# The second attention's last two key heads: folding their weights at the third head instead of beside the feed-forward

## The chip, the cores and the metric

The kernel runs on one NeuronCore of a Trainium2 chip. A core has a matmul engine (TensorE, called PE in the profile), a vector engine (VectorE, DVE), a scalar engine (ScalarE, ACT), a general one (GpSimd, POOL) and SyncE (SP), which here only issues DMAs. Each engine works through its own queue in order, and semaphores tie the queues together. PE writes only to PSUM, and ACT or DVE has to copy from there.

The metric is the device time of one execution in microseconds; the median of a few runs is compared. The profile is one further execution with the hardware profiler on, so its times sum to its own time.

## The reference

Two decoder layers on x of 4 x 256 tokens of width 256, each a gated cross-attention to a context (4 x 1601 tokens of width 128) and a gated feed-forward:

```python
x = x + tanh(g_xattn[0]) * L0_xattn(layernorm(x), ctx)   # 16 heads of 16
x = x + tanh(g_ffn[0])   * L0_ffn(layernorm(x))          # 16 experts, 8 chosen per token, and a shared one
x = x + tanh(g_xattn[1]) * L1_xattn(layernorm(x), ctx)   # 16 query heads of 128, 8 key heads
x = x + tanh(g_ffn[1])   * L1_ffn(layernorm(x))          # weights rounded to -1, 0, 1 times a scale
```

The second attention, which the change is about:

```python
q = (x @ Wq) in 16 heads of 128;  k, v = (ctx @ Wk), (ctx @ Wv) in 8 heads of 128, each for 2 query heads
attn = softmax(mask(q @ k.T / sqrt(128)))
out = concat(attn @ v) @ Wo
```

Since k = ctx Wk, a head's scores are x (Wq_h Wk^T) ctx^T, and since v = ctx Wv, its output is (attn ctx) (Wv Wo_h). The kernel makes the two small products once per head ("folding"): aq (256 x 128) and vo (128 x 256), and attends to ctx itself.

## The kernel before

The kernel runs in four stages, one after the other: first attention, first feed-forward (from 536 us on), second attention (from 638 us on), second feed-forward. Within a stage a Python loop writes the instructions out, and `keep_order` ties every engine to that order, except SP in the first feed-forward.

**First feed-forward.** It takes 512 tokens at a time ("half") and 16 experts for each, so 32 experts' turns, called slots 0 to 31. A turn (`expert`) is three products on PE into PSUM (`ps_v` L1279, `ps_g` L1280, `ps_w` L1281), a ReLU on ACT (L1235), two products on DVE (L1239, L1241) and one on POOL (L1242), which gives hT. After each second expert `add_pair` multiplies the previous pair's hT by the third weight (L1293). Other work is put beside the experts by slot, in the table `beside`: layer norms, routing, the second attention's context and mask (`prepare_ctx`, `prepare_mask`), the output tiles (L1303, L1304), and `fold_steps`, the folding of the second attention's weights.

**Folding.** A query head takes two steps. The first, called A in the text that follows, transposes the head's two blocks of Wq (L1211) and, for the first of the two query heads of a key head, also Wk and Wv (L1214) into one PSUM tile; ACT copies them out as kvT (L1216) and, scaled, qwT (L1218). The second, B, makes the two blocks of aq (L1224) and vo (L1227) in another PSUM tile; ACT copies aq (L1228), DVE vo (L1229). The 32 steps of 16 heads stand in slots 6 to 32, five slots with two. Wk, Wv and Wq are loaded to the memory of the first attention's keys (`space`), Wo to a tile of its own (`wo1`), by SP (L1182 to L1187); the context follows on the same queue (`ctxT`, L1192).

**Second attention.** Its units are (batch, head), 64 in all. The loop over v works on several at a time: the scores of unit v in eight tiles (PE L1457; DVE subtracts from the mask and finds the extremum, L1464; ACT takes the exponential, L1472), then the softmax factors (`weigh_sets`: DMAs L1483 to bring the parts of a query together, DVE L1486 and L1488, ACT L1489, DVE L1492 to L1495, DMAs L1498 back), then POOL multiplies (L1507), DVE transposes (`turn`, L1513), PE sums over the context (`attend`, L1520), ACT copies (`take`, L1530) and PE projects with vo (`project_out`, L1538). `project(v + 2)` (L1446, copied by ACT at L1447) makes the queries two units ahead, in one of two PSUM buffers named `ps_m`. The DMAs L1483 and L1498 are issued half by SP and half by ACT. For the first three units nothing is left to sum yet, or only little: at v = 2 PE finishes the third head's scores and goes on to the first head's sums, which need the first head's transposes.

At v = 2 the order on ACT is: the exponentials of the third head, the two DMAs L1483, the exponential L1489, two DMAs L1498, `take`, the copy of the queries. On DVE the transposes of the first head stand behind the score tiles of the third one.

In the background the loop quantises the last stage's weights: `fetch` loads 512 columns at a time into `w_q` (two buffers), one step every second unit, from v = 5 on.

Of the kernel before, what the change touches and what calls it, by code (L numbers as in the profile page):

```python
# [9 lines left out]
F32 = mybir.dt.float32  # L10
# [3 lines left out]
AF = mybir.ActivationFunctionType  # L14
# [7 lines left out]
P = 128  # L22
B, S, D = 4, 256, 256
NT = B * S // P
QT = S // P
DC = D // P
# [6 lines left out]
H = 16  # L33
# [26 lines left out]
def tile_gated_cross_blocks(ctx: ExitStack, tc: tile.TileContext, a: dict, out: bass.AP):  # L60
# [1072 lines left out]

    def prepare_ctx(b, pst, tag):

        cx = contexts[b] = l1w.tile([P, NB1, P], F32, name="cx1", bufs=2)
        for g0 in range(0, NB1, 4):
            n = min(4, NB1 - g0)
            cg = l1w.tile([P, 4, SETS, TQ], F32, name="cg")
            for i in range(SETS):  # L1140
                k0 = i * KS + g0 * TQ
                nc.gpsimd.tensor_copy(
                    cg[:, :n, i, :], ctxT[b][:, k0 : k0 + n * TQ].rearrange("p (k q) -> p k q", q=TQ)
                )
# [28 lines left out]
    with ExitStack() as ph:  # L1173
        began = len(nc.cur_bb.bb.instructions)
        space = kTs_f[(B - 1) % 2]
        at1 = NKV * HD1
        wk1, wv1 = space[:, :at1], space[:, at1 : 2 * at1]
        wq1 = space[:, 2 * at1 : 2 * at1 + DC * H * HD1].rearrange("p (c n) -> p c n", c=DC)
        fp = ph.enter_context(tc.tile_pool(name="l1f", bufs=1))
        ft = ph.enter_context(tc.tile_pool(name="l1ft", bufs=2))  # L1180
        wo1 = fp.tile([P, H, D], F32, name="wo1")
        nc.sync.dma_start(out=wk1, in_=a["L1_xattn_Wk"])  # L1182
        nc.sync.dma_start(out=wv1, in_=a["L1_xattn_Wv"])
        for h in range(0, H, 4):
            cols = slice(h * HD1, (h + 4) * HD1)
            nc.sync.dma_start(out=wq1[:, :, cols], in_=a["L1_xattn_Wq"].rearrange("(c p) n -> p c n", p=P)[:, :, cols])
            nc.sync.dma_start(out=wo1[:, h : h + 4], in_=a["L1_xattn_Wo"].rearrange("(h p) n -> p h n", p=P)[:, h : h + 4])  # L1187
            if h == 4:
                first_mask = prepare_mask(0)
                next(first_mask)  # L1190
        for b in range(B):
            nc.sync.dma_start(out=ctxT[b][:, :S2], in_=a["ctxT"][:, b, :])  # L1192
            nc.gpsimd.memset(ctxT[b][:, S2:], 0.0)
# [10 lines left out]
        def fold_steps():  # L1204
            for kv in range(NKV):
                cols = slice(kv * HD1, (kv + 1) * HD1)
                for r in range(GRP):
                    h = kv * GRP + r
                    pt = ps_x.tile([P, 512], F32, name="ps_x")
                    for c in range(DC):  # L1210
                        nc.tensor.transpose(pt[:, c * P : (c + 1) * P], wq1[:, c, h * HD1 : (h + 1) * HD1], ident)  # L1211
                    if r == 0:
                        for i, w in enumerate((wk1, wv1)):
                            nc.tensor.transpose(pt[:, (DC + i) * P : (DC + i + 1) * P], w[:, cols], ident)  # L1214
                        kvT = ft.tile([P, 2, P], F32, name="kvT")
                        nc.scalar.copy(kvT.rearrange("p i c -> p (i c)"), pt[:, DC * P :])  # L1216
                    qwT = ft.tile([P, DC, P], F32, name="qwT")
                    nc.scalar.activation(  # L1218
                        qwT.rearrange("p c d -> p (c d)"), pt[:, : DC * P], AF.Copy, scale=1.0 / math.sqrt(HD1)
                    )  # L1220
                    yield
                    pm = ps_x.tile([P, 512], F32, name="ps_x")
                    for c in range(DC):
                        nc.tensor.matmul(  # L1224
                            pm[:, c * P : (c + 1) * P], lhsT=qwT[:, c, :], rhs=kvT[:, 0, :], start=True, stop=True
                        )
                    nc.tensor.matmul(pm[:, DC * P :], lhsT=kvT[:, 1, :], rhs=wo1[:, h, :], start=True, stop=True)  # L1227
                    nc.scalar.copy(aq[:, :, h, :], pm[:, : DC * P].rearrange("p (c d) -> p c d", c=DC))  # L1228
                    nc.vector.tensor_copy(vo[:, h, :], pm[:, DC * P :])  # L1229
                    yield  # L1230
# [85 lines left out]
        follow(fold_steps(), sorted([*range(6, 33), 7, 14, 17, 22, 25]))  # L1316
# [23 lines left out]
        for step in beside.pop(32):  # L1340
            step()
# [15 lines left out]
    with ExitStack() as ph:  # L1357
# [20 lines left out]
        def quantise():  # L1378
# [4 lines left out]
            def fetch(k):  # L1383
                i, j = todo[k % len(todo)]
                w = got[k] = ap.tile([P, FC], F32, name="w_q", bufs=2)
# [5 lines left out]

            asum = small.tile([P, len(todo)], F32, name="asum", bufs=1)
# [17 lines left out]
            for k, (i, j) in enumerate(todo):  # L1410
# [3 lines left out]
                below = ap.tile([P, FC], F32, name="q_dn")  # L1414
# [173 lines left out]
        for v in range(len(units) + 8):  # L1588
# [13 lines left out]
            if v - 3 in made:  # L1602
                project_out(v - 3)
            if v - 2 in made:
                if early:
                    for half in range(2):
                        turn(v - 2, half)
                for k in range(NB1):
                    attend(v - 2, k)
# [133 lines left out]
```

## Time and profile before

| what | value |
|---|---|
| median of 3 runs | 1567.58 us (1565.86 to 1568.48) |
| the profiled execution's own time | 1567.33 us |
| its span | 1565.6 us |
| PE busy | 1523.9 us, 97% |
| DVE, ACT, POOL busy | 71%, 51%, 36% |
| mean granted clock of PE | 0.995 |
| share of PE in the chain that ended last | 88% |

Times in the timeline are microseconds from the start of the span. A row is a run of instructions of one line and shape: start, time, engine, line, operation, tiles, shapes, count, and in brackets how long the engine had been idle before and what ended that. A matmul's time includes the way through the array, so that the next one starts before it ends; where instructions follow closely, the distance from one start to the next is what an instruction costs. A row of a table of windows has the bounds of the stretch, its length, the busy time of PE, PEld (weight loads), DVE, ACT and POOL with the number of instructions, the granted clock of PE (1.00 is full), the busy share of the DMA engines, and GB/s.

### The profile page before, as it was taken

The page shows a single profiled execution, that of the slowest core. Times are in us where ns is not written, and L with a number is a line of the kernel's source. Part 1 is how long each engine was busy: PE and PEld are TensorE (multiplying, and loading weights), DVE is VectorE, ACT ScalarE, POOL GpSimd, SP SyncE. Part 2 cuts the span into 40 slices and gives each one's busy share as a digit, 9 for nine tenths or more (in the row PEclk, how much of TensorE's full clock was granted, in tenths as well). Part 3 has the DMA queues.
Part 4 walks back from the last instruction along what each step waited for, and adds up shares of the span by engine and source line. Part 5 has one row for each costly group of instructions (what it writes and reads, how often), then busy time and mean ns, then how long its engine had stood idle before and what let it go on. Part 6 is the DMA issues. An engine that isn't in the chain of part 4 may idle for free.

```text
span 1565.6 us, 31791 instructions
## 1 busy us (share of the span) xinstructions
PE 1523.9 (97%) x12210; PEld 924.1 (59%) x12218; DVE 1104.2 (71%) x2559; ACT 795.4 (51%) x2017; POOL 563.1 (36%) x454
## 2 busy tenths in 40 slices
PE   8999999999999999899999999999999999999998
PEld 5455555555555544366666666666666666666655
DVE  7666676676567367677777777777787777777655
ACT  4456556566555544534445445454445554454343
POOL 4142022032012245244445444454444544444400
PEclk9999999999999999999999999999999999999999
DMA  5120003003200410000000000000000000000000
GB/s 144 24 51 1 1 2 64 1 2 56 46 15 15 146 54 1 2 2 15 9 23 8 16 10 15 9 15 9 9 16 9 22 9 16 9 2 2 2 0 28
DMA packets 47596, 34.48 MB, mean 22 GB/s; under 512 B 31058, under 2 KB 42196, under 8 KB 47316
## 3 DMA queue, kind: packets, MB, share of 16 engines
q1 hardware_dynamic: 33732, 31.22, 8.2%
q10 hardware_dynamic: 13712, 1.23, 0.6%
q8 instruction: 96, 1.57, 0.4%
q14 instruction: 56, 0.46, 0.1%
HBM read 30.16 MB, written 1.46 MB: 20 GB/s over the span
## 4 chain that ended last, share of the span: by engine, by line
PE 88%; DVE 4%; ACT 4%; issue 2%; POOL 1%; DMA 1%; ACTq 0%; SPq 0%; DVEq 0%; POOLq 0%
PE ps_o L1520 21%; PE ps_sc L1457 20%; PE ps_s L801 9%; PE ps_g L758 7%; PE ps_o L827 7%; PE ps_y L1538 4%; PE ps_m L1446 3%; PE ps_v L1279 2%; ACT pr L1472 1%; PE ps_m L586 1%; PE ps_a L1293 1%; ACT e L812 1%; PE ps_m L493 1%; PE ps_m L734 1%; PE ps_g L1651 1%
## 5 line engine op out<-in xcount | busy, mean ns | idle before, releaser
L1507 POOL TENSOR_TENSOR pr<-pr,rs 128x1604 f32<-128x1604 f32 x128 | 364.0, 2865 | 434.1 <-DMA rs<-ws 387.8
L1520 PE MATMUL ps_o<-pT,cx 128*128 128x256 f32 x1664 | 371.5, 381 | 8.6 <-DVE pT L1513 8.6
L1457 PE MATMUL ps_sc<-ctxT,qT 128*32 128x401 f32 x4096 | 359.7, 502 | 0.5 <-DVE nm L1464 0.5
L1464 DVE CUSTOM_DVE_ANT_0 pr<-ps_sc,mk 128x401 f32<-128x401 f32 x512 | 293.8, 576 | 88.7 <-PE ps_sc L1457 50.6
L1472 ACT ACTIVATE pr<-pr,nm 128x401 f32<-128x401 f32 x512 | 321.1, 628 | 69.0 <-DVE nm L1464 68.5
L1520 PEld LDWEIGHTS ps_o<-pT,cx 128*128 128x128 f32 x1664 | 317.8, 191 | 52.6 <-DVE pT L1513 9.7
L812 ACT ACTIVATE e<-ps_s 128x512 f32<-128x512 f32 x430 | 222.3, 565 | 166.6 <-PE ps_s L801 158.1
L767 DVE TENSOR_REDUCE mxs<-ps_g 128x1 f32<-128x453 f32 x372 | 216.5, 623 | 112.1 <-PE ps_s L801 81.0
L801 PE MATMUL ps_s<-qT,kT 32*128 32x256 f32 x1600 | 250.8, 403 | 11.2 <-ACT e L812 9.9
L1457 PEld LDWEIGHTS ps_sc<-ctxT,qT 128*32 128x32 f32 x4096 | 126.5, 110 | 204.4 <-issue 120.5
L1513 DVE STREAM_TRANSPOSE pT<-pr 128x1664 f32<-128x1664 f32 x128 | 242.9, 1899 | 5.4 <-POOL pr L1507 5.3
L758 PE MATMUL ps_g<-kT,qT 32*128 32x453 f32 (+1 forms) x992 | 244.0, 539 | 1.4 <-DVE mxs L767 1.1
L801 PEld LDWEIGHTS ps_s<-qT,kT 32*128 32x128 f32 x1600 | 151.6, 185 | 89.6 <-ACT e L812 49.1
L1489 ACT ACTIVATE ws<-ws 32x32 f32<-32x32 f32 x64 | 14.6, 228 | 198.7 <-DVE ws L1488 198.7
L827 PE MATMUL ps_o<-e,vp 128*32 128x256 f32 x1664 | 114.3, 388 | 0.0
L1530 ACT COPY ao<-ps_o 128x256 f32<-128x256 f32 x64 | 23.8, 372 | 151.9 <-PE ps_o L1520 130.2
L1472 ACT ACTIVATION_READ_ACCUMULATOR pr<-pr,nm 128x1 f32 x512 | 95.5, 187 | 0.0
L758 PEld LDWEIGHTS ps_g<-kT,qT 32*128 32x128 f32 x992 | 90.0, 184 | 8.4 <-DVE mxs L767 7.7
L827 PEld LDWEIGHTS ps_o<-e,vp 128*32 128x32 f32 x1664 | 43.4, 110 | 62.1 <-issue 45.5
L1538 PE MATMUL ps_y<-vo,ao 128*128 128x256 f32 x256 | 72.4, 405 | 0.1
L1538 PEld LDWEIGHTS ps_y<-vo,ao 128*128 128x128 f32 x256 | 43.4, 189 | 44.4 <-ACT pr L1472 39.8
L1486 DVE TENSOR_REDUCE low<-bq 32x8 f32<-32x32 f32 x64 | 12.4, 194 | 75.9 <-DMA bq<-nm 75.9
(325 smaller groups left out, 1533.8 us busy)
## 6 DMA issues: line engine op xcount, KB each, us to landing
kT<-by_head SPq DMA_DIRECT2D x64, 93.3 KB, 4.6
ctxT<-in_ctxT_dram SPq DMA_DIRECT2D x4, 800.5 KB, 9.8
ctx<-in_ctxT_dram SPq DMA_DIRECT2D x12, 199.0 KB, 4.7
kT<-in_L_xattn_Wq_dram SPq DMA_DIRECT2D x4, 512.0 KB, 3.6
wo<-in_L_xattn_Wo_dram SPq DMA_DIRECT2D x4, 512.0 KB, 5.2
bq<-nm SPq DMA_DIRECT2D x128, 2.0 KB, 1.7
bq<-nm ACTq DMA_DIRECT2D x128, 2.0 KB, 2.0
rs<-ws SPq DMA_DIRECT2D x128, 1.0 KB, 1.9
```

What stands on the lines that cost most here:

```text
L758: nc.tensor.matmul(ps[:, m * w : (m + 1) * w], lhsT=qT[rows, ii * P : (ii + 1) * P], rhs=kT[rows, s // 2, n * CW0 : n * CW0 + w], start=Tr ...
L767: nc.vector.tensor_reduce(mx[:, i, r + k, n : n + 1], ps[:, :w], AX.X, ALU.max)
L801: nc.tensor.matmul(ps[:, jj * S : (jj + 1) * S], lhsT=kT[rows, s // 2, (j + jj) * P : (j + jj + 1) * P], rhs=qT[rows], start=True, stop=True,)
L812: nc.scalar.activation(e[:, k, : nj * S], ps[:, : nj * S], AF.Exp)
L827: nc.tensor.matmul(summed[u][(r + k) * W : (r + k + 1) * W, :S], lhsT=vps[b % 2][:, t, h * VW : h * VW + W], rhs=made[u, j, r][:, k, jj * ...
L1457: nc.tensor.matmul(ps[i * TQ : (i + 1) * TQ, :KS], lhsT=queries[u][:, t * TQ : (t + 1) * TQ], rhs=ctxT[b][:, i * KS : (i + 1) * KS], start ...
L1464: nc.vector.tensor_tensor_reduce(out=prs[u % 3][:, t, :KS], in0=ps[:, :KS], in1=masks[b], scale=-1.0, scalar=3.0e38, op0=ALU.add, op1=ALU. ...
L1472: nc.scalar.activation(p, p, AF.Exp, bias=found[u][:, 0, t : t + 1], scale=-1.0, accum_out=found[u][:, 1, t : t + 1])
L1507: nc.gpsimd.tensor_tensor(p, p, bc_last(factors[:, ts], KS), ALU.mult)
L1513: nc.vector.transpose(pTs[u % 2][:, ts].rearrange("p t k -> p (t k)"), prs[u % 3][:, ts].rearrange("p t k -> p (t k)"))
L1520: nc.tensor.matmul(po[:, u % 2], lhsT=contexts[b][:, k, :], rhs=pTs[u % 2].rearrange("p t (k q) -> p t k q", q=TQ)[:, :, k, :], start=k == ...
L1538: nc.tensor.matmul(ys[b][:, i], lhsT=outs[u][:, i * P : (i + 1) * P], rhs=vo[:, h, :], start=(h, i) == (0, 0), stop=(h, i) == (H - 1, QT - 1),
```

## The change

The weights of the last two key heads (four of the sixteen query heads, `LATE` = 2) are loaded to tiles of their own (`lkv`, `lq`, `lo`) and folded in the second attention's loop at v = 2, between the third head's scores and the first head's sums. For these four heads the fold's PSUM tiles are `ps_m`, its copies kvT and qwT have one buffer, and ACT copies vo too. The other twelve heads are folded beside the feed-forward as before, 24 steps in slots 6 to 8 and 10 to 30. Half of Wo (eight heads) now lies in `space` too. The quantising uses `lq` and `lkv` in place of `w_q` and `q_dn`.

```diff
+    LATE = 2
+    late = l1_stack.enter_context(tc.tile_pool(name="late", bufs=1, side="right"))
+    lkv = late.tile([P, 2, LATE, HD1], F32, name="lkv")
+    lq = late.tile([P, DC, LATE * GRP, HD1], F32, name="lq")
+    lo = late.tile([P, LATE * GRP, D], F32, name="lo")
+
+    def load_late():
+        h0, kv0 = H - LATE * GRP, NKV - LATE
+        for i, n in enumerate(("Wk", "Wv")):
+            nc.sync.dma_start(
+                out=lkv[:, i], in_=a[f"L1_xattn_{n}"][:, kv0 * HD1 :].rearrange("p (h n) -> p h n", n=HD1)
+            )
+        for c in range(DC):
+            nc.sync.dma_start(
+                out=lq[:, c],
+                in_=a["L1_xattn_Wq"][c * P : (c + 1) * P, h0 * HD1 :].rearrange("p (h n) -> p h n", n=HD1),
+            )
+        nc.sync.dma_start(out=lo, in_=a["L1_xattn_Wo"].rearrange("(h p) n -> p h n", p=P)[:, h0:])
+
+    def fold(kv, r, kT_of, q_of, o_of, pst, tag, pool, memo):
+
+        h = kv * GRP + r
+        pt = pst.tile([P, 512], F32, name=tag)
+        for c in range(DC):
+            nc.tensor.transpose(pt[:, c * P : (c + 1) * P], q_of(c, h), ident)
+        if r == 0:
+            for i in range(2):
+                nc.tensor.transpose(pt[:, (DC + i) * P : (DC + i + 1) * P], kT_of(i, kv), ident)
+            memo[kv] = pool.tile([P, 2, P], F32, name="kvT")
+            nc.scalar.copy(memo[kv].rearrange("p i c -> p (i c)"), pt[:, DC * P :])
+        kvT = memo[kv]
+        qwT = pool.tile([P, DC, P], F32, name="qwT")
+        nc.scalar.activation(qwT.rearrange("p c d -> p (c d)"), pt[:, : DC * P], AF.Copy, scale=1.0 / math.sqrt(HD1))
+        yield
+        pm = pst.tile([P, 512], F32, name=tag)
+        for c in range(DC):
+            nc.tensor.matmul(pm[:, c * P : (c + 1) * P], lhsT=qwT[:, c, :], rhs=kvT[:, 0, :], start=True, stop=True)
+        nc.tensor.matmul(pm[:, DC * P :], lhsT=kvT[:, 1, :], rhs=o_of(h), start=True, stop=True)
+        nc.scalar.copy(aq[:, :, h, :], pm[:, : DC * P].rearrange("p (c d) -> p c d", c=DC))
+        eng = nc.scalar.copy if kv >= NKV - LATE else nc.vector.tensor_copy
+        eng(vo[:, h, :], pm[:, DC * P :])
+        yield
...
-        for h in range(0, H, 4):
+        for h in range(0, HE, 4):
             cols = slice(h * HD1, (h + 4) * HD1)
             nc.sync.dma_start(out=wq1[:, :, cols], in_=a["L1_xattn_Wq"].rearrange("(c p) n -> p c n", p=P)[:, :, cols])
-            nc.sync.dma_start(out=wo1[:, h : h + 4], in_=a["L1_xattn_Wo"].rearrange("(h p) n -> p h n", p=P)[:, h : h + 4])
+            nc.sync.dma_start(out=wo1[h // 8][:, h % 8 : h % 8 + 4], in_=a["L1_xattn_Wo"].rearrange("(h p) n -> p h n", p=P)[:, h : h + 4])
             if h == 4:
                 first_mask = prepare_mask(0)
                 next(first_mask)
+        load_late()
...
-        follow(fold_steps(), sorted([*range(6, 33), 7, 14, 17, 22, 25]))
+        follow(fold_steps(), [*range(6, 9), *range(10, 31)])
...
-                w = got[k] = ap.tile([P, FC], F32, name="w_q", bufs=2)
+                w = got[k] = w_q[:, k % 2]
...
+            w_q = lq.rearrange("p c h n -> p (c h n)").rearrange("p (k n) -> p k n", n=FC)
+            below = lkv.rearrange("p i h n -> p (i h n)")
...
-                below = ap.tile([P, FC], F32, name="q_dn")
...
             if v - 3 in made:
                 project_out(v - 3)
+            if v == 2:
+                memo = {}
+                for kv in range(NKV - LATE, NKV):
+                    k = kv - (NKV - LATE)
+                    for r in range(GRP):
+                        for _ in fold(
+                            kv, r,
+                            lambda i, kv: lkv[:, i, k],
+                            lambda c, h: lq[:, c, h - (H - LATE * GRP)],
+                            lambda h: lo[:, h - (H - LATE * GRP)],
+                            ps_m, "ps_m", ap, memo,
+                        ):
+                            pass
             if v - 2 in made:
```

More of the change, by code (lines that the diff above doesn't have):

```diff
@@ L1175, in tile_gated_cross_blocks @@
         space = kTs_f[(B - 1) % 2]
-        at1 = NKV * HD1
+        HE = H - LATE * GRP
+        at1, at2 = HE // GRP * HD1, 2 * (HE // GRP) * HD1 + DC * HE * HD1
         wk1, wv1 = space[:, :at1], space[:, at1 : 2 * at1]
-        wq1 = space[:, 2 * at1 : 2 * at1 + DC * H * HD1].rearrange("p (c n) -> p c n", c=DC)
+        wq1 = space[:, 2 * at1 : at2].rearrange("p (c n) -> p c n", c=DC)
         fp = ph.enter_context(tc.tile_pool(name="l1f", bufs=1))
         ft = ph.enter_context(tc.tile_pool(name="l1ft", bufs=2))
-        wo1 = fp.tile([P, H, D], F32, name="wo1")
-        nc.sync.dma_start(out=wk1, in_=a["L1_xattn_Wk"])
-        nc.sync.dma_start(out=wv1, in_=a["L1_xattn_Wv"])
-        for h in range(0, H, 4):
+        wo1 = [
+            space[:, at2 : at2 + 8 * D].rearrange("p (h n) -> p h n", n=D), fp.tile([P, HE - 8, D], F32, name="wo1")
+        ]
+        nc.sync.dma_start(out=wk1, in_=a["L1_xattn_Wk"][:, :at1])
+        nc.sync.dma_start(out=wv1, in_=a["L1_xattn_Wv"][:, :at1])
+        for h in range(0, HE, 4):
             cols = slice(h * HD1, (h + 4) * HD1)
             nc.sync.dma_start(out=wq1[:, :, cols], in_=a["L1_xattn_Wq"].rearrange("(c p) n -> p c n", p=P)[:, :, cols])
-            nc.sync.dma_start(out=wo1[:, h : h + 4], in_=a["L1_xattn_Wo"].rearrange("(h p) n -> p h n", p=P)[:, h : h + 4])
+            nc.sync.dma_start(out=wo1[h // 8][:, h % 8 : h % 8 + 4], in_=a["L1_xattn_Wo"].rearrange("(h p) n -> p h n", p=P)[:, h : h + 4])
             if h == 4:
@@ L1204, in fold_steps @@
         def fold_steps():
-            for kv in range(NKV):
-                cols = slice(kv * HD1, (kv + 1) * HD1)
+            memo = {}
+            for kv in range(NKV - LATE):
                 for r in range(GRP):
[L1208 to L1219, printed above, removed]
-                    )
[L1221 to L1230, printed above, removed]
+                    yield from fold(
+                        kv, r,
+                        lambda i, kv: (wk1, wv1)[i][:, kv * HD1 : (kv + 1) * HD1],
+                        lambda c, h: wq1[:, c, h * HD1 : (h + 1) * HD1],
+                        lambda h: wo1[h // 8][:, h % 8, :],
+                        ps_x, "ps_x", ft, memo,
+                    )
         def squared_relu_times(dst, pg, pv, pw=None):
@@ L1339, in tile_gated_cross_blocks @@
             waiting = (half, e, hTs)
-        for step in beside.pop(32):
+        for step in beside.pop(32, []):
             step()
@@ L1603, in tile_gated_cross_blocks @@
                 project_out(v - 3)
+            if v == 2:
+                memo = {}
+                for kv in range(NKV - LATE, NKV):
+                    k = kv - (NKV - LATE)
+                    for r in range(GRP):
+                        for _ in fold(
+                            kv, r,
+                            lambda i, kv: lkv[:, i, k],
[4 more added lines that the diff above has]
+                            pass
             if v - 2 in made:
```

## The prediction

> **What bounds the kernel now.** I read the busy shares first, then who TensorE waited for, then the two stretches that the change touches, in order of time. TensorE (PE) is busy 97% of the span, so a stretch of it costs what it does there plus what it waits there. From the page:
>
> ```profile
> PE 1523.9 (97%) x12210; PEld 924.1 (59%) x12218; DVE 1104.2 (71%) x2559; ACT 795.4 (51%) x2017; POOL 563.1 (36%) x454
> ```
>
> Only one wait of PE in the second attention is large (line; total us, times, longest):
>
> ```profile
> PE ps_o L1520 <- DVE pT L1513: 8.6, 2, 8.1
> ```
>
> The timeline shows it between the third head's scores (L1457) and the first sums (L1520). In brackets is the idle time and what ended it; the last row is the same work one head later.
>
> ```profile
> 655.51 5.59 PE L1457 MATMUL ps_sc<-ctxT,qT 128*32 128x401 f32 x64
> 669.16 7.60 PE L1520 MATMUL ps_o<-pT,cx 128*128 128x256 f32 x26 [8.06 <-DVE pT L1513]
> 684.05 5.78 PE L1520 MATMUL ps_o<-pT,cx 128*128 128x256 f32 x26
> ```
>
> PE ends at 661.10 and starts at 669.16, 8.06 us. The first sums take about 2 us more than the next ones (7.60 in the chain against 5.61), and the windows say why: the clock (the last but two column here) had fallen.
>
> ```profile
> 661.00:665.00 4.00, 0.10 (x4) 0.00 (x0) 3.08 (x9) 3.73 (x13) 2.25 (x1) 1.00 0.00 0
> 665.00:669.00 4.00, 0.00 (x0) 0.00 (x0) 4.00 (x4) 0.72 (x2) 1.16 (x1) 0.61 0.04 2
> 669.00:673.00 4.00, 3.83 (x10) 3.10 (x11) 2.77 (x4) 0.23 (x1) 4.00 (x2) 0.54 0.01 1
> ```
>
> From 674 on PE never waits for long, so what is later at the end of the first sums (676.76) is later at the end of the kernel. The question is when ScalarE (ACT), which has to empty every PSUM tile of the fold, gets to it in this gap. ACT in the timeline:
>
> ```profile
> 649.36 1.48 ACTq L1483 DMA_DIRECT2D bq<-nm  x2
> 650.88 0.37 ACT L1447 COPY qT<-ps_m 128x256 f32<-128x256 f32 x1 [1.56 <-PE ps_sc L1457]
> ...
> 667.02 0.19 ACT L1472 ACTIVATION_READ_ACCUMULATOR pr<-pr,nm 128x1 f32 x1
> 667.24 1.42 ACTq L1483 DMA_DIRECT2D bq<-nm  x2
> ```
>
> ACT works on the third head's exponentials until 667.21 and then issues two DMAs, which hold it for 1.42 us: after the issue at 649.36 the next copy starts at 650.88, though its matmul had ended at 649.0. So ACT is free at 668.66, 7.6 us after the scores and half a microsecond before PE's wait ends.
>
> **What is removed from the feed-forward.** A head is two steps: A, transposes of Wq (and Wk, Wv for a key head's first query head), and B, three products. PE from one start to the next:
>
> ```profile
> 618.84 0.44 PE L1211 MATMUL ps_x<-ident,kT 128*128 128x128 f32 x2
> 619.12 0.38 PE L134 MATMUL ps_x<-ident,xn 128*128 128x128 f32 x2
> ...
> 621.71 0.71 PE L1224 MATMUL ps_x<-kvT,qwT 128*128 128x128 f32 x4
> 622.26 0.60 PE L1227 MATMUL ps_x<-wo,kvT 128*128 128x256 f32 x2
> 622.69 0.38 PE L134 MATMUL ps_x<-ident,xn 128*128 128x128 f32 x2
> ...
> 624.27 0.44 PE L1211 MATMUL ps_x<-ident,kT 128*128 128x128 f32 x2
> 624.55 0.38 PE L1214 MATMUL ps_x<-ident,kT 128*128 128x128 f32 x2
> 624.86 1.08 PE L1293 MATMUL ps_a<-hT,kT 128*64 128x512 f32 x4
> ...
> 632.37 1.79 PE L1293 MATMUL ps_a<-hT,kT 128*64 128x512 f32 x4
> ```
>
> A is 0.28 us for a second head, 0.59 for a first one; B is 0.98. Four heads are 2 x 0.59 + 2 x 0.28 + 4 x 0.98 = 5.7 us. Not all of it is saved. The last head's A and B (slots 31 and 32) lie in the shadow of the last expert's chain: PE ends its product at 629.56, then follow ACT, DVE and POOL (its product ends at 633.03), and only then the last L1293, whose 1.79 us is mostly waiting. Taking 0.28 + 0.98 us from there makes PE wait longer. So 15 heads in slots 6 to 30 become 12: 2 x 0.59 + 0.28 + 3 x 0.98 = 4.40 us saved.
>
> Is PE the limit in those slots? An expert without any filler ran at 1.63 us (starts at 538.48, 540.11, 541.78, each 0.20 to 0.23 us of waiting for DVE); with filler it is 1.27 plus the filler. Every slot keeps a step or other work, the smallest being A with 1.27 + 0.28 + 0.09, and odd slots have L1293 (1.0 us) as well. So 4.40 holds, at worst 2.4 if DVE, busy 69% at 600 to 620, holds two slots per head. DVE's four vo copies (0.33 us each) go; they bound nothing.
>
> Loads: the same bytes in three more DMAs on SP's queue. The five late ones wait for the transposes at 532.2 (L866) and are issued in SP's idle time before 535.67, ahead of the last Wo part, the mask and ctxT on that queue. After 535.67 SP then issues one Wo part instead of four at about 0.5 us each, so ctxT, first read at 552.14 on POOL, comes no later. POOL's order is unchanged. The second attention's quantising reads the same amounts into lq instead of w_q, with two halves as before; its only new wait is for transposes long done. Cost: 0. Without this cover a late ctxT would hold POOL, and each hT behind it, one for one.
>
> **What is added at the third head.** All on PE and ACT, in their written order, 14 ACT instructions between the DMAs at 667.24 and the factors' exponential (L1489). PE does the first A at once, 661.1 to 661.9, and then waits for ACT. ACT's pace and the way from B to the copy are those beside the feed-forward:
>
> ```profile
> 554.10 0.71 PE L1224 MATMUL ps_x<-kvT,qwT 128*128 128x128 f32 x4
> ...
> 555.28 0.37 ACT L1228 COPY aq<-ps_x 128x256 f32<-128x256 f32 x1 [0.65 <-PE ps_x L1227]
> 555.55 0.39 ACT L1218 ACTIVATE qwT<-ps_x 128x256 f32<-128x256 f32 x1
> ```
>
> B's start to the aq copy is 1.18 us; copies start 0.27 apart; qwT takes 0.39 and PE follows 0.05 later. kvT at 668.70, qwT 668.97, so B of the first head starts at 669.41. From one B to the next: 1.18 + 0.27 (aq) + 0.27 (vo, now on ACT too) + 0.44 = 2.16 us, and 0.27 more for kvT at a new key head, 2.43. PE's transposes for the next head fit between. The four: 669.41 + 2.16 + 2.43 + 2.16 + 0.98 = 677.14, PE free for the first sums. They are no longer hidden by the gap: nearly all of the fold comes after its end.
>
> The clock adds to it. In the trace it falls at about 665.9 whatever follows, so the first B runs at half speed: by transposes at that clock (four in 1.04 us at 53.43, against 0.53) and sums (0.43 us against 0.22) B takes 1.96 and the copy comes 1.03 later. How long it stays low no row shows, since PE is here busy only about 75% of each 2.3 us. At the least one head is slow, 1.03 us; with two, and the four transposes between them (0.46 more), 2.5; with all four, 4.6. The Trainium skill (TensorE: Matmul & The Clock Gate, "The HAM clock gate") has full speed return after a window of about 3.4 us of sustained activity, and be lost after an idle one. The rows agree for solid work: 669.16 to 672.66, 3.5 us. But they also show a stretch that wasn't idle and lost it:
>
> ```profile
> 47.90:51.40 3.50, 1.34 (x6) 0.67 (x6) 1.29 (x5) 2.65 (x7) 0.00 (x0) 1.00 0.03 7
> 51.40:54.90 3.50, 3.48 (x20) 2.35 (x24) 1.29 (x3) 1.37 (x3) 0.00 (x0) 0.51 0.00 0
> ```
>
> 38% busy was too little. Read strictly, "sustained" keeps the clock low through the fold and into the sums; 75% is nearer to solid work than to 38%, so I take 1.6 us, between one and two heads. The sums then start at 678.7 and run at full speed, 5.61, to 684.3, against 676.76: 7.6 us later.
>
> Queued behind the fold on ACT is L1489 (670.77 before, some 679.6 now). DVE waits there at L1492, and behind that are the transposes of the second head and the DMA of the third head's factors, for which POOL waits. The second head's transposes then end at 684.5, and its sums are due at 684.3 + 0.86 + 5.52 + 1.06 = 691.7, so nothing more is late.
>
> Sum: -4.4 + 7.6 = +3.2 us against the profiled execution's 1567.33 (span 1565.6), which is 0.25 below the median of the runs: 1570.5 there, 1570.8 as a median.
>
> **Rivals.**
> - The clock stays low through the fold: 677.14 + 4.6 + 7.60 = 689.3, 12.6 later, less 4.4: +8.2, 1575.8. For it: the 38% row. Against it: the fold's PE is nearly twice as busy.
> - The feed-forward saves only 2.4 because DVE and ACT set the pace: +5.2, 1572.8. Against it: PE shows no wait from 560 to 620.
> - Not slower: a DMA issue doesn't hold ACT's copies. Then kvT starts at 667.24 and all is 1.42 earlier: +1.8, 1569.4. Against it: three pairs like 649.36 and 650.88.
> - Faster, the gap takes the fold: ACT would serve the copies between the exponentials, and the 4.4 us are a plain gain, 1563.2. It decides if the fold ends before 675.55 (676.76 + 4.4 - 5.61), 3.1 us earlier than I have it. Against it: ACT's order, in which the copies stand behind the exponentials and the DMAs.
>
> **How the numbers follow.** This kernel's measurement tells about 0.2%, 3.1 us, from no change; the forecast lies on that edge. Main case 60% (1569.8 to 1572.0, half on each side), low clock 15%, slow feed-forward 10%, early copies 7%, faster 6%, anything else 2%. Slower: 30 + 15 + 10 + 2 = 57%; same 29 + 7 = 36%; faster 7%. The range leaves out the faster case and the upper half of the low clock: 1568.2 to 1575.5.
>
> **What would show it.** Right: PE shows the first transposes right after the third head's scores and then a wait of about 7 us for ACT; the first fold copy starts 1.4 us after the last exponential; four heads about 2.2 to 3.2 us apart; the first sums in 5.6 us, not 7.6; the feed-forward 4.4 us shorter. Wrong: copies before the DMA issue, a clock at 0.5 up to the sums, new waits of PE for DVE in the feed-forward, or the second head's sums waiting for DVE.

## The result, and the profile after

The changed kernel takes 1572.78 us (median of 7 runs, 1572.16 to 1574.05) against 1567.58 (7 runs beside it, 1565.61 to 1568.48): a ratio of 1.0037, 95% interval 1.0026 to 1.0049. It is slower by more than the 0.2% that this kernel's measurement can tell. The profiled execution took 1572.16 us, with a span of 1570.4.

The busy shares of the page have hardly moved, so they say nothing of the cause:

```profile
PE 1525.9 (97%) x12210; PEld 924.4 (59%) x12218; DVE 1101.0 (70%) x2555; ACT 796.9 (51%) x2021; POOL 563.2 (36%) x454
```

The largest wait of PE in the second attention has a new place. In the list of waits (line; total us, times, longest), 9.4 us now lie ahead of the fold's products, 7.4 of them in one piece, and the 8.1 us wait of the first sums for DVE is 0.5:

```profile
PE ps_m L1170 <- ACT qwT L1166: 9.4, 4, 7.4
PE ps_o L1553 <- DVE pT L1546: 0.5, 1, 0.5
```

PE's timeline at the third head (L1490 scores, L1158 and L1161 transposes, L1170 and L1171 products of the fold, L1553 sums):

```profile
650.64 5.59 PE L1490 MATMUL ps_sc<-ctxT,qT 128*32 128x401 f32 x64
656.17 0.44 PE L1158 MATMUL ps_m<-ident,lq 128*128 128x128 f32 x2
656.44 0.38 PE L1161 MATMUL ps_m<-ident,lkv 128*128 128x128 f32 x2
664.26 1.23 PE L1170 MATMUL ps_m<-kvT,qwT 128*128 128x128 f32 x4 [7.44 <-ACT qwT L1166]
...
667.37 1.22 PE L1170 MATMUL ps_m<-kvT,qwT 128*128 128x128 f32 x4 [0.60 <-ACT qwT L1166]
...
671.04 1.23 PE L1170 MATMUL ps_m<-kvT,qwT 128*128 128x128 f32 x4 [0.75 <-ACT qwT L1166]
...
674.15 1.22 PE L1170 MATMUL ps_m<-kvT,qwT 128*128 128x128 f32 x4 [0.60 <-ACT qwT L1166]
...
676.01 6.71 PE L1553 MATMUL ps_o<-pT,cx 128*128 128x256 f32 x26
682.56 1.03 PE L1479 MATMUL ps_m<-xnT,aq 128*128 128x256 f32 x4
```

PE does the first transposes at once, then waits until ACT has copied them. The four heads begin 3.11, 3.67 and 3.11 us apart, where 2.16, 2.43 and 2.16 had been worked out. ACT shows why the first copy is late and, in its brackets, what stretches the rest:

```profile
661.88 0.19 ACT L1505 ACTIVATION_READ_ACCUMULATOR pr<-pr,nm 128x1 f32 x1
662.10 1.41 ACTq L1516 DMA_DIRECT2D bq<-nm  x2
663.55 0.37 ACT L1163 COPY kvT<-ps_m 128x256 f32<-128x256 f32 x1 [1.48 <-issue]
...
666.38 0.37 ACT L1172 COPY aq<-ps_m 128x256 f32<-128x256 f32 x1 [2.17 <-PE ps_m L1171]
```

The last exponential, two DMA issues, then the copies. Within the fold, however, ACT waits 2.17 us for PE in each head, where it waits 1.24 us in the run below that keeps the full clock (the prediction went by the 0.65 beside the feed-forward). PE is slow because of its clock (the last but two column; rows of one window of 3.41 us each, laid on the clock's own changes at 660.82 and 677.89):

```profile
657.41:660.82 3.41, 0.00 (x0) 0.00 (x0) 3.25 (x10) 2.28 (x9) 1.00 (x1) 1.00 0.00 0
660.82:664.23 3.41, 0.00 (x0) 0.00 (x0) 3.14 (x2) 1.38 (x4) 1.52 (x1) 0.50 0.05 3
664.23:667.65 3.42, 2.79 (x9) 2.10 (x10) 0.83 (x2) 0.94 (x3) 3.42 (x2) 0.50 0.02 5
667.65:671.06 3.41, 2.66 (x11) 1.97 (x11) 0.00 (x0) 1.31 (x4) 0.74 (x1) 0.50 0.00 0
671.06:674.47 3.41, 2.81 (x9) 2.12 (x10) 0.00 (x0) 0.94 (x3) 0.00 (x0) 0.50 0.00 0
674.47:677.89 3.42, 3.42 (x11) 2.88 (x11) 0.74 (x5) 0.76 (x3) 0.00 (x0) 0.50 0.00 0
```

After a window in which PE did nothing the clock falls to half. It stays there through three windows of the fold in which PE was busy 78 to 82% (2.66 to 2.81 of 3.41 us), and comes back after the first window with no hole, the one that holds the last products and the first sums.

In the feed-forward there are two new waits of PE, one for DVE in slot 10 and one for POOL at the end:

```profile
563.67 0.69 PE L1310 MATMUL ps_v<-xlT,kT 64*128 64x512 f32 x1 [0.36 <-DVE val_g L1272]
...
628.13 1.07 PE L1324 MATMUL ps_a<-hT,kT 128*64 128x512 f32 x2 [1.09 <-POOL hT L1273]
```

The whole execution, cut at the same places of PE's timeline (the first expert's product; the first product of the queries after the feed-forward; the end of the third head's scores; the first sums; the next product of the queries), in us:

| stretch | before | after | difference |
|---|---|---|---|
| up to the first expert (first attention) | 536.94 | 535.36 | -1.58 |
| feed-forward | 101.03 | 97.64 | -3.39 |
| to the end of the third head's scores | 23.13 | 23.23 | +0.10 |
| from there to the first sums | 8.06 | 19.78 | +11.72 |
| the first sums | 7.44 | 6.55 | -0.89 |
| the rest | 889.0 | 887.9 | -1.1 |
| span | 1565.6 | 1570.4 | +4.8 |

So the change takes 3.39 us out and puts 10.83 in, and 2.7 us come from places that it doesn't touch. What those are worth is a question for the experiments too.

### The profile page after: what moved, and what is told of

Same layout as the page of the kernel before. It is cut to its first block, busy times and chain, and to the rows that moved or that the text cites. A ratio compares the mean times of both kernels' runs of the same rounds, so it can differ in the third digit from the quotient of the medians.

```text
span 1570.4 us, 31798 instructions
## 1 busy us (share of the span) xinstructions
PE 1525.9 (97%) x12210; PEld 924.4 (59%) x12218; DVE 1101.0 (70%) x2555; ACT 796.9 (51%) x2021; POOL 563.2 (36%) x454
## 3 DMA queue, kind: packets, MB, share of 16 engines
q10 hardware_dynamic: 13712, 1.23, 0.6%
## 4 chain that ended last, share of the span: by engine, by line
PE 89%; DVE 4%; ACT 3%; issue 2%; POOL 1%; DMA 0%; ACTq 0%; SPq 0%; DVEq 0%; POOLq 0%
PE ps_o L1553 22%; PE ps_sc L1490 21%; PE ps_s L801 9%; PE ps_g L758 7%; PE ps_o L827 7%; PE ps_y L1571 4%; PE ps_m L1479 3%; PE ps_v L1310 2%; PE ps_m L586 1%; ACT e L812 1%; PE ps_a L1324 1%; ACT pr L1505 1%; PE ps_m L493 1%; PE ps_m L734 1%; PE ps_g L1697 1%
## 5 line engine op out<-in xcount | busy, mean ns | idle before, releaser
L1553 PE MATMUL ps_o<-pT,cx 128*128 128x256 f32 x1664 | 370.6, 380 | 0.5 <-DVE pT L1546 0.5
L1490 PE MATMUL ps_sc<-ctxT,qT 128*32 128x401 f32 x4096 | 359.5, 502 | 0.5 <-DVE nm L1497 0.5
L1505 ACT ACTIVATE pr<-pr,nm 128x401 f32<-128x401 f32 x512 | 321.0, 628 | 69.5 <-DVE nm L1497 68.6
L1553 PEld LDWEIGHTS ps_o<-pT,cx 128*128 128x128 f32 x1664 | 316.9, 190 | 44.2 <-DVE pT L1546 0.9
L1490 PEld LDWEIGHTS ps_sc<-ctxT,qT 128*32 128x32 f32 x4096 | 126.3, 110 | 204.3 <-issue 120.7
L1505 ACT ACTIVATION_READ_ACCUMULATOR pr<-pr,nm 128x1 f32 x512 | 95.4, 186 | 0.0
L1479 PE MATMUL ps_m<-xnT,aq 128*128 128x256 f32 x256 | 65.8, 380 | 0.0
```

The source lines that it names most:

```text
L1490: nc.tensor.matmul(ps[i * TQ : (i + 1) * TQ, :KS], lhsT=queries[u][:, t * TQ : (t + 1) * TQ], rhs=ctxT[b][:, i * KS : (i + 1) * KS], start ...
L1505: nc.scalar.activation(p, p, AF.Exp, bias=found[u][:, 0, t : t + 1], scale=-1.0, accum_out=found[u][:, 1, t : t + 1])
L1553: nc.tensor.matmul(po[:, u % 2], lhsT=contexts[b][:, k, :], rhs=pTs[u % 2].rearrange("p t (k q) -> p t k q", q=TQ)[:, :, k, :], start=k == ...
```

## The experiments

All ratios are to the kernel before, which ran on the same chip in each batch (medians 1565.9 to 1567.4). The changed kernel stands at 1.0037. The theory: the fold's work is free for PE, but ACT reaches it only when the wait that it was meant to fill is over, and the wait's half clock then stretches it. Rivals: ACT's copies alone set its pace, whatever the clock; ACT is full there, so that the order of the work doesn't matter; the feed-forward's saving is smaller than counted and explains the loss.

**The feed-forward alone.**

```
+        nc.gpsimd.memset(aq[:, :, H - LATE * GRP :, :], 0.0)
+        nc.gpsimd.memset(vo[:, H - LATE * GRP :, :], 0.0)
...
-            if v == 2:
-                memo = {}
-                for kv in range(NKV - LATE, NKV):
...
```

> The changed kernel without the fold of the last four heads at the third head; their folded weights are set to zero, so those four heads' output is left out. What remains of the change is the shorter feed-forward. By the prediction's count (4.40 us of TensorE work gone) 1567.6 - 4.4 = 1563.2. By the trace after, in which the stretch from the first fold step to the last output tile went from 85.72 to 82.34 us, 1567.6 - 3.4 = 1564.2. If the feed-forward's pace were set by VectorE and ScalarE (the rival in the prediction), 1565.2. The 8 us wait ahead of the first sums and their slow 7.6 us should be there again.

The kernel leaves out the four heads' fold, and with it their output. Measured: 1563.14 us, ratio 0.9974 (0.9965 to 0.9983), 4.1 us less than before. Its trace has the feed-forward at 97.63 us, the same 3.4 saved as in the changed kernel, and behind the scores the old wait and the slow sums:

```profile
665.96 7.84 PE L1555 MATMUL ps_o<-pT,cx 128*128 128x256 f32 x26 [7.76 <-DVE pT L1548]
```

The median agrees with the count of 4.4, the trace with 3.4; the trace decides for this stretch, since the rest of the span (887.9 us) is 1.1 shorter here as well. The feed-forward's part is a gain, and what costs is the fold at the third head.

**The addition alone.**

```
-            for kv in range(NKV - LATE):
+            for kv in (*range(NKV - LATE), 0, 1):
-        follow(fold_steps(), [*range(6, 9), *range(10, 31)])
+        follow(fold_steps(), sorted([*range(6, 33), 7, 14, 17, 22, 25]))
```

> The changed kernel with the feed-forward given its old number of fold steps back: it folds the first four heads a second time (same result) in the 32 slots of the kernel before, and the last four are folded at the third head as in the change. This is the change's addition alone. If the two parts add, the feed-forward takes 101.0 us again instead of 97.6 (first expert product to first query product), the third head stays at 26.3 us from the scores' end to the end of the sums, and the kernel takes 1572.8 + 3.4 = 1576.2. If the shorter feed-forward had moved the second attention's clock or its transfers, the third head's stretch changes too.

Measured: 1579.48 us (4 runs, 1574.93 to 1580.21), ratio 1.0080 (1.0061 to 1.0098). The feed-forward takes 101.03 us, to the hundredth what it took before, and the third head 26.50 from the scores' end to the end of the sums. So the parts add in the two stretches. The median is 3.3 us above what was expected: the expected sum started from the changed kernel's median, whose trace has short times outside the two stretches; in this kernel's trace the first attention took 536.96 us and the rest 889.4, together 3.1 more.

**A slot moved.**

```
-        follow(fold_steps(), [*range(6, 9), *range(10, 31)])
+        follow(fold_steps(), [*range(6, 30)])
```

> The changed kernel with the same 24 fold steps in slots 6 to 29 instead of 6 to 8 and 10 to 30: slot 9 is filled, slot 30 isn't. In the trace after, TensorE waits 0.43 us longer at the expert behind slot 9 and 10, for VectorE's product of expert 9, which the kernel before had covered with a fold step. If that hole is why the feed-forward saved 3.4 us and not the 3.9 that its steps cost, it now takes 97.2 us instead of 97.64; if the wait is VectorE's pace and only moves, 97.6. A kernel 0.4 us shorter is below what the medians tell, so the trace decides.

The feed-forward took 97.62 us: no change (one run, 1574.06). The wait for DVE is still there, 0.32 us:

```profile
565.74 0.69 PE L1310 MATMUL ps_v<-xlT,kT 64*128 64x512 f32 x1 [0.32 <-DVE val_g L1272]
```

It belongs to DVE's pace at that point, where the routing's steps stand beside the experts, and not to the empty slot. In the traces of before and after, expert by expert, a slot is shorter by 0.94 us where a B is gone, 0.45 for a first head's A, 0.22 for a second head's: 3 x 0.94 + 2 x 0.45 + 0.22 = 3.94. With the wait in slot 10 (0.43 us more at that expert) 3.5 are left, near the 3.39 measured.

**ACT without the DMA issues.**

```
-                QUEUES[i % 2].dma_start(out=by_query[:, i], ...
+                QUEUES[0 if u == 2 else i % 2].dma_start(out=by_query[:, i], ...
```

> The changed kernel, with the third head's four transfers of its minima and sums all issued by SP, so that ScalarE has no DMA to issue between its last exponential and the fold's first copy. If the issue holds ScalarE (1.41 us in the trace after), the first fold copy starts 0.1 us after the last exponential instead of 1.5, and everything behind it is 1.4 us earlier: 1571.4 against 1572.8. If the issue doesn't hold it (a rival in the prediction), no change. The factors' exponential behind the fold comes no later, so nothing is lost elsewhere.

SP issues all four transfers of the third head's minima and sums. Measured: 1572.01 us, ratio 1.0029 (1.0020 to 1.0037), 0.8 us less than the changed kernel in the medians, inside the intervals of both. The trace shows both halves of the answer. The first product now comes 6.2 us after the scores instead of 8.0; about 1.5 of these 1.9 us are the issue (ACT's first copy follows its last exponential at once), so the issue did hold ACT. But the clock keeps half speed to 679.6, into the sums, which take 7.48 us instead of 6.55. Rows of single windows of the clock:

```profile
672.78:676.19 3.41, 2.81 (x10) 2.21 (x9) 0.00 (x0) 1.06 (x4) 0.00 (x0) 0.50 0.00 0
676.19:679.61 3.42, 3.42 (x9) 2.70 (x8) 2.65 (x6) 0.64 (x3) 0.00 (x0) 0.50 0.02 1
```

The first window without a hole begins 0.36 us after the sums do, and the clock waits for its end. Of the 1.9 us won 0.9 were given back; how much is given back hangs on where the windows happen to lie.

**The wait filled, twice too much.** Matmuls whose result nobody reads, on PE between the fold's first transposes and its first products; in the second of the two kernels WARM is (30, 3, 2, 3), so that some stand between the heads too:

```
+                WARM = (30, 0, 0, 0)
...
+                            if n == 0:
+                                for _ in range(WARM[k * GRP + r]):
+                                    nc.tensor.matmul(po[:, 1], lhsT=ident, rhs=ctxT[0][:, :S], start=True, stop=True)
```

> The changed kernel with 30 matmuls of 128x256 whose result nobody reads, put on TensorE between the fold's first transposes and its first products, 6.5 us at full clock, to keep the clock up through the 7.4 us wait. Inside the fold nothing is added: there TensorE has about 5.7 us of work in 7.7. Theory (low clock stretched the fold from 7.7 to 11.75 us and the sums from 5.61 to 6.55): if such a fold is dense enough to keep the clock, 5.0 us less than the changed kernel, 1567.8. If the clock is lost again inside the fold, between 1 and 4 us less, 1569 to 1572. Rival (ScalarE's copies set the fold's pace, whatever the clock): no change, 1572.8.

> As the kernel with 30 matmuls in the wait, and 3, 2 and 3 more of them ahead of the products of the second, third and fourth head, which fills the 0.6 to 0.75 us waits of TensorE for ScalarE. Theory (low clock): full clock throughout, 5.0 us less than the changed kernel, 1567.8. Rival (ScalarE's copies alone): 1572.8. If this one keeps the clock and the one without the fillers between the heads doesn't, the short waits inside the fold are what loses it.

Measured: 1574.05 us (1.0040, 1.0026 to 1.0054) and 1574.54 (1.0043, 1.0028 to 1.0057). Neither brought its 5 us, and the fault was the size of the filler: an fp32 matmul here is two passes, 0.43 us and not 0.215, so that 30 of them held the fold up to 673.5, 5.6 us after ACT's copy was done. The trace is of use all the same: at full clock the fold took 7.67 us from the first product to the sums without fillers between the heads. That it can keep the clock by itself called for the run at the right size.

**The wait filled to fit.** Half as many of them, against the kernel with 30:

```
-                WARM = (30, 0, 0, 0)
+                WARM = (15, 0, 0, 0)
```

> The changed kernel with half as many of the unread matmuls between the fold's first transposes and its first products: 15. In the run with 30 each took 0.43 us (two passes of 0.215), twice what was counted, so that they held up the fold by 5.6 us; yet with them the fold ran from its first product to the sums in 7.67 us and the sums in 5.61. Now 15 x 0.43 = 6.5 us lie inside the wait of 7.4. Theory (the low clock stretched fold and sums): 11.75 + 6.55 - 7.67 - 5.61 = 5.0 us less than the changed kernel, 1567.8. Rival (ScalarE's copies set the fold's pace and the shorter fold of the last run came from copies that were done long before): first product to sums still 11 to 12 us, 1572 to 1573.

Measured: 1569.36 us (20 runs, 1567.19 to 1572.48), ratio 1.0016 (1.0009 to 1.0024): less than half of the loss is left. The trace has the 5.0 us of the theory to a tenth: 7.77 us from the fold's first product to the sums instead of 11.75, and sums of 5.61 instead of 6.55.

```profile
660.53 6.64 PE L1652 MATMUL ps_o<-ctxT,ident 128*128 128x256 f32 x30
667.89 0.71 PE L1170 MATMUL ps_m<-kvT,qwT 128*128 128x128 f32 x4 [0.71 <-ACT qwT L1166]
...
674.67 0.71 PE L1170 MATMUL ps_m<-kvT,qwT 128*128 128x128 f32 x4 [0.81 <-ACT qwT L1166]
...
675.66 5.78 PE L1553 MATMUL ps_o<-pT,cx 128*128 128x256 f32 x26
```

ACT's copies are the same ones, and the first product comes 7.8 us behind the scores, as good as before. The rival that ACT's copies set the pace whatever the clock has fallen. The median gained less (3.4 us); the lowest times of the two kernels are 5.0 apart (1567.19 and 1572.16). The profiled run had four windows at half clock in the first attention, at 51 to 65 us, which the change and this edit don't touch: that stretch took 539.23 us here and 535.36 in the changed kernel's trace. Such windows would account for the median, but only profiled runs show them.

**Only the short waits filled.** One unread matmul of 128x192 ahead of the products of the second, third and fourth head; the long wait stays, so the fold begins at half clock:

```
+                            if n == 0 and (k, r) != (0, 0):
+                                nc.tensor.matmul(po[:, 1, :192], lhsT=ident, rhs=ctxT[0][:, :192], start=True, stop=True)
```

> The changed kernel with one unread matmul of 128x192 (about 0.65 us at half clock) ahead of the products of the second, third and fourth head, which fills the 0.60 to 0.75 us in which TensorE waits there; the wait of 7.4 us before the fold is left as it is, so that the fold begins at half clock. In the trace after, the clock stayed at half speed from 661.2 to 678.2 although TensorE was busy 83% of the fold. If the short waits are what kept it there, the clock comes back 3.4 to 6.8 us after the first product, the fold takes about 9 to 10 us instead of 11.75 and the sums 5.6: 2.5 to 4 us less, 1569 to 1570. If something else kept it there (the transposes not counting as work, or the weight loads), no gain: 1572.8 to 1573.3.

and three transposes in its place:

```
+                                for _ in range(3):
+                                    nc.tensor.transpose(po[:, 1, :P], ident, ident)
```

> The same with three unread 128x128 transposes (about 0.64 us at half clock) in each place instead of the matmul. The Trainium skill (TensorE: Matmul & The Clock Gate) says of transposes that they don't count as TensorE activity in the same way. If so here, this run stays at half clock through the fold where the run with the matmuls gets its clock back, and costs 1572.8 to 1573.5. If transposes count like matmuls, it does what the run with the matmuls does.

Measured: 1570.29 us (20 runs), ratio 1.0023 (1.0016 to 1.0030), and 1570.88 (14 runs), 1.0019 (1.0011 to 1.0027). Both get the clock back after one window, and with it a sum of 5.61 us; the way from the scores' end to the sums is 17.39 and 16.98 us instead of 19.78. The windows of the first, on the clock's changes at 665.8 and 672.6:

```profile
665.82:669.23 3.41, 1.07 (x5) 1.07 (x6) 2.58 (x4) 0.81 (x4) 2.63 (x1) 0.50 0.05 8
669.23:672.64 3.41, 3.41 (x12) 2.63 (x12) 0.27 (x1) 0.94 (x3) 3.05 (x2) 0.50 0.00 0
672.64:676.06 3.42, 2.88 (x18) 2.07 (x16) 0.00 (x0) 1.73 (x6) 0.00 (x0) 1.00 0.00 0
```

A single filler of 0.85 us at half clock, which closed the 0.6 us hole, made the difference: 3.41 of 3.41 brings the clock back where 2.82 didn't. And the transposes did what the matmuls did, so these fp32 transposes count as activity in this kernel: in the full window of that run they are 1.2 of the 3.41 us, and without them it would be no fuller than windows that left the clock at half.

**The kernel before with its wait filled.**

```
+            if v == 2:
+                for _ in range(16):
+                    nc.tensor.matmul(po[:, 1], lhsT=ident, rhs=ctxT[0][:, :S], start=True, stop=True)
```

> The kernel before, with 16 unread matmuls of 128x256 (6.9 us) in the 8.06 us wait ahead of the first sums and nothing else. If the clock's fall in that wait costs what the timeline shows, the first sums take 5.6 us instead of 7.6 and the kernel 2.0 us less, 1565.5. If the clock does no harm here, no change, 1567.5.

Measured: 1565.06 us (13 runs), ratio 0.9989 (0.9981 to 0.9997). The first sums take 5.72 us instead of 7.44. So the wait in the kernel before costs 1.7 us more than its own length.

**The same fold in another order.**

```
+        def spread():
+            step = once(late_steps())
+            step()
+            for t in range(6):
+                scores(2, t)
+                if t < 4:
+                    exponentials(2, t)
+            next(shares[1])
+            scores(2, 6)
+            next(shares[1])
+            scores(2, 7)
+            multiply(1)
+            step()
+            step()
+            exponentials(2, 4)
+            exponentials(2, 5)
+            step()
+            step()
+            exponentials(2, 6)
+            step()
+            step()
+            exponentials(2, 7)
+            step()
...
-                QUEUES[i % 2].dma_start(out=factors[...
+                QUEUES[0 if u == 1 else i % 2].dma_start(out=factors[...
```

`late_steps` gives the eight steps of the four heads; the first `step()` is the first head's A, ahead of the scores.

> The changed kernel with the same fold of the last four heads in another order: the first transposes go on TensorE ahead of the third head's scores, and on ScalarE the fold's copies are put between the third head's exponentials (four of these, then the copies of the first head, two exponentials, and so on) instead of behind all eight; the second head's factors are sent by SP alone, so that ScalarE has no DMA to issue in the stretch. Theory (what makes the fold dear is that ScalarE reaches it when the wait is over): fold and wait overlap, the sums start about 8.2 us after the scores' end instead of 19.8, at full or nearly full clock: 1560 to 1562. If the clock falls all the same, 2 us more. If the exponentials that now come later delay the second head's sums: up to 4 us more, 1566. Rival (ScalarE is full in this stretch, so any order costs what the fold costs): 1568 to 1571.

Measured: 1562.84 us (8 runs, 1560.23 to 1564.85), ratio 0.9973 (0.9962 to 0.9983): faster than both kernels, by 0.27% than the one before. On ACT the fold's copies now stand between the exponentials (L1505):

```profile
657.41 0.63 ACT L1505 ACTIVATE pr<-pr,nm 128x401 f32<-128x401 f32 x1
...
658.59 0.34 ACT L1172 COPY aq<-ps_m 128x256 f32<-128x256 f32 x1
658.84 0.36 ACT L1174 COPY vo<-ps_m 128x256 f32<-128x256 f32 x1
659.11 0.37 ACT L1166 ACTIVATE qwT<-ps_m 128x256 f32<-128x256 f32 x1
659.38 0.61 ACT L1505 ACTIVATE pr<-pr,nm 128x401 f32<-128x401 f32 x1
```

and PE goes from the scores straight into the products, with a longest wait of 1.59 us:

```profile
656.58 0.71 PE L1170 MATMUL ps_m<-kvT,qwT 128*128 128x128 f32 x4
...
659.53 0.71 PE L1170 MATMUL ps_m<-kvT,qwT 128*128 128x128 f32 x4 [1.59 <-ACT qwT L1166]
...
665.13 5.78 PE L1553 MATMUL ps_o<-pT,cx 128*128 128x256 f32 x26
```

The sums start 8.49 us after the scores' end, 0.4 later than in the kernel before without any fold there, and at full clock (5.61 us). The ratio is that of the feed-forward alone, 0.9974, in which these four heads weren't folded at all: in this order they cost nothing that the times show. The rival that ACT is full here has fallen; the order was what made the fold dear. The same edit takes ACT's two issues for the second head's factors away, which was not tried alone; two issues taken from ACT in the run above brought 0.8 us. The second head's sums weren't delayed.

**The kernel before once more.**

> The kernel before once more, for a second trace of it: which of the differences outside the two stretches that the change touches (1.6 us in the first attention, 0.3 us at the 35th head, 0.8 us after the last heads) are the same in it, and which come and go from run to run. If they come and go, some of them will be absent here.

One run, 1568.22 us. With the trace of the kernel before whose wait was filled there are three of that kernel. What they show of the places that the change doesn't touch:

- First attention: 536.94, 536.52 and 536.51 us. In all fourteen traces that stretch goes with its windows at half clock: 535.3 with none (the changed kernel, the reordered one, the one with the transposes), 536.5 with one at 506 us, 537 with two at 51 to 74 us, 539.2 with four from 51 to 65. It comes and goes, so the 1.58 us are chance.
- The feed-forward of the kernel before: 101.0, 102.6 and 104.0 us. The two longer ones have one and two windows at half clock from 543 us on, right after PE's waits for DVE at the fourth and fifth expert. None of the eleven traces of the changed kernels has them. The same experts leave a window there just as empty in the trace of the changed kernel (PE busy 2.07 of 3.41 us, at full clock after it) as in the one that lost the clock (2.13), so it isn't shown that the change keeps them away.
- The 0.29 us at the 35th head are in the first trace alone: DVE waited 2.92 us there for the transfer of the head's minima, 1.23 us in the changed kernel.
- The last heads and the output: 888.9 to 889.1 us for the rest, against 887.9 in nine of the eleven traces of changed kernels (888.5 and 889.4 in the others). The last heads move with the transfer of their minima, for which DVE waited 1.5 us in the changed kernel and 3.0 where the rest took 889.4. About 0.5 us of it lies behind PE's last matmul, in the output's transfers (6.3 to 6.7 us from PE's end to the span's end before, 5.8 to 5.9 after). Why is open. It is in all of them, and it was not tried what part of the change brings it.

## Why the prediction was right

The sign, the range (1568.2 to 1575.5) and the order of the terms held: a small gain in the feed-forward, a fold that ACT delays until the gap is over, and a clock that makes it dearer. The value, 1570.8, was 2.0 us short, and 1572.78 lies above the main case (1569.8 to 1572.0). Two of the signs that it named for being wrong came true: half clock up to the sums, and a new wait of PE for DVE in the feed-forward. By its steps:

- **ACT's order and the DMA issue: right.** The first product was put 8.31 us after the scores' end and came at 8.03; the first copy follows the last exponential by the 1.41 us of the issues. The run with ACT free of them moved it 1.9 us ahead, about 1.5 of that by the issue. The rival in which the issue holds nothing is out.
- **The fold's pace at full clock: right.** Predicted 7.73 us from the first product to the sums; 7.67 and 7.77 in the two runs that filled the wait and nothing else.
- **The clock: mis-sized.** "75% is nearer to solid work than to 38%, so I take 1.6 us, between one and two heads", and sums at full speed. Measured: 11.75 - 7.77 = 4.0 us in the fold and 6.55 - 5.61 = 0.9 in the sums, 4.9 in all. This is the term that failed. What a slow head costs was worked out well (1.03 us, and 0.46 for the transposes between heads; 0.9 to 1.2 per head measured); how many are slow was not: all four, and the first half of the sums. The rule that stood beside it, that full speed returns after a window of about 3.4 us of sustained activity (the Trainium skill, TensorE: Matmul & The Clock Gate, "The HAM clock gate"), read strictly gave 4.6 for the fold and was the better guide: windows 78 to 82% busy did not bring the clock back, and at this place a full one did in every trace. The 38% row spoke of losing the clock; getting it back asked for more, and the estimate put the two on one scale. (The 7.60 us that the prediction sets against 5.61 run to the end of the last sum; by the distance to the next product, as the 5.61, they are 7.44.)
- **The feed-forward: 4.40 predicted, 3.39 measured.** An A was costed by the distance from its first transposes to the next instruction, 0.28 and 0.59 us; taking it away brought 0.22 and 0.45, and a B 0.94 for 0.98. That is 0.46 us of the difference. The wait for DVE in slot 10 is most of the rest. The rival named DVE's pace for it, at a price of 2.0 us; the mechanism is there at one slot.
- **Loads, quantising, and what is behind the fold: right, cost 0.** The second head's sums weren't late, and the heads from the fourth to the 34th stand on the same hundredths in both traces.

Together: +0.1, -3.39 and +10.83 make +7.5 where +3.2 had been predicted. The medians differ by 5.2 (the ratio says 4.1 to 7.7), nearer to the prediction than the terms are, because of 2.7 us from elsewhere, as far as the two traces speak for the medians: 1.6 of first attention and 0.3 at the 35th head are chance, the rest is unexplained. The lowest times of the two kernels are 6.6 us apart (1565.61 and 1572.16). So it was partly luck that the number came this near with the clock's term 3.3 us too small. (Among the chances, half of the 60% and 7% make 37% for no change, not 36.) The low-clock rival (1575.8) had the right mechanism for the fold; it was too high by the fold (4.6 for 4.0) and the sums, which it took at 7.60 throughout (6.55), and by those 2.7 us, and too low by the 1.0 us that the feed-forward didn't save.

## What to carry to other kernels

A wait of one engine is a place for work only if every engine that the work needs is free during it: ask where the work stands in the order of the engine that empties PSUM, and put its copies between that engine's other instructions, not behind them. Placed behind, four heads cost 10.8 us; spread among the exponentials, nothing. And count the clock with a wait: at the third head the work behind a wait of TensorE of 5.6 us or more began at half clock in every trace, and stayed there until it filled a window of 3.4 us without a hole, so that closing a 0.6 us hole with a dummy paid for itself.

## What the runs showed of the hardware

- At the third head, losing the clock and getting it back asked for different amounts of work. It was lost in nine traces, each time after a window of 3.41 us without any work of PE. From half clock, windows with 2.66 to 2.82 us of work kept it at half (three in a row in each of four traces, among them the changed kernel and the one with ACT freed), and in all nine a window of 3.41 of 3.41 released it. At full clock a window with much less kept it: in the reordered kernel and in the one with the wait filled to fit,

```profile
657.96:661.37 3.41, 1.58 (x10) 1.25 (x10) 3.31 (x10) 3.08 (x13) 0.42 (x1) 1.00 0.01 0
```

```profile
669.16:672.58 3.42, 1.75 (x12) 1.32 (x11) 0.07 (x1) 2.06 (x7) 2.85 (x2) 1.00 0.00 0
```

  46 and 51% busy and no loss (their bounds are counted in periods from changes of the clock elsewhere in the same trace).
- Elsewhere PE's busy share doesn't decide it. In the first attention, where many products use 32 rows or columns of the array (`32*128` and `128*32` in the timeline), four traces came back to the full clock only after four windows, though PE was busy all the time in at least the second and the third. Those two, in the run with the short waits filled by matmuls:

```profile
54.84:58.25 3.41, 3.41 (x20) 2.38 (x20) 2.45 (x8) 1.41 (x3) 2.11 (x5) 0.50 0.01 2
58.25:61.66 3.41, 3.41 (x24) 1.64 (x23) 2.53 (x6) 1.08 (x2) 2.96 (x4) 0.50 0.00 0
```

  Five other traces came back there after one.
  In the trace of the kernel before with its wait filled the clock fell at 506.4 us after a full window,

```profile
502.95:506.37 3.42, 3.42 (x36) 2.46 (x32) 1.77 (x7) 1.19 (x4) 0.00 (x0) 1.00 0.00 0
```

  and at 543.9 us after one with 2.13 us of the experts' products (`64*128` and `128*64`), while the first trace of the kernel before kept it with 2.10 at the same experts. So the full window that released the clock at the third head is no rule for products that use less of the array. Whether such products count for less was not tried; what counts as busy is open.
- The clock changes at multiples of one period: low for 17.07 us in the changed kernel, five times 3.41. Where these windows lie differs from run to run, so that the same instructions fall into other windows. The spread of the runs goes with the clock: those of the kernel with the wait filled to fit go from 1567.2 us at a mean granted clock of 0.999 to 1572.5 at 0.996.
- The fp32 transposes here count as activity for the clock like matmuls. The Trainium skill (TensorE: Matmul & The Clock Gate, "Part 4: PE-mode transpose") says that transposes don't count in the same way; the run with three of them in each hole says that these do. The page's figures are for bf16, and the profile doesn't show whether these run in the mode that it speaks of.
- An fp32 matmul of 128x256 takes two passes, 0.43 us at full clock in a row of them.
- Two DMA issues hold ACT for 1.41 us, and four on SP cost ACT nothing.
